# Score steps of 384 and 128 columns in one hold of PSUM banks, and another order of the attention's round

## The chip, the core and the metric

The kernel runs on one core of a Trainium2 chip. The metric is the device time of one execution in microseconds (us). The engines are named as in the profile: PE is TensorE (PEld its weight loads), DVE is VectorE, ACT is ScalarE, POOL is GpSimd, and SP is SyncE, which issues most of the DMAs. `L579` means line 579 of the kernel.

## The reference, cut to what matters

The program is a macaron block over x of 2 x 1024 rows of 256: half a feed-forward network (FFN), causal attention, and the same FFN again. The FFN with its 2:4 sparsity is left out here, since the change does not touch it.

```
q = (x @ Wq + bq) -> 32 heads of 8;  k, v = ... -> 8 heads of 8     # B = 2, T = 1024
q = q * cos + rotate_half(q) * sin;  k the same
k_rep, v_rep = repeat(k, 4), repeat(v, 4)                            # 4 query heads share one k, v
scores = einsum('bhqd,bhkd->bhqk', q, k_rep) / sqrt(8)
scores = where(kpos > qpos, -inf, scores)
attn = softmax(scores)
out = einsum('bhqk,bhkd->bhqd', attn, v_rep) @ Wo + bo
```

## The kernel before

The first FFN runs with the projections of sequence 0 between its steps, then come the attention and the second FFN. The attention is worked in 16 units, one for each sequence `b` and key head `g`; a unit has four query heads, taken as two pairs. It goes through three stages.

- **Pass 1** (`pass1`, L544) makes the scores of a block of 128 queries `qt` against up to 512 keys `kc`, with the queries on the partitions, and finds each row's maximum. The two heads of a pair lie in two strips of 64 rows of TensorE and write to the two banks of one buffer. On a diagonal block four or eight small bf16 matmuls (L567) add the causal mask. VectorE then reduces the buffer to a negated maximum for each row and head (L579). Queries 0 to 511 (half 0) need one step each, and the later ones (half 1) two, whose results `negated` (L582) joins on VectorE (L587). GpSimd splits the maximum into a high and a low part (L397, L398).
- **Shift** (`shift`) turns the split maxima with four small matmuls (L598) into rows, ScalarE copies them out (L606), and SP writes them into two extra rows of the transposed queries with four DMAs (L609). From then on a score matmul delivers the score less its row's maximum.
- **Pass 2** (`pass2`, L625 to L646) makes the scores again, for a block of 128 keys `kb` against up to 512 queries of a half `qh`, now with the keys on the partitions. ScalarE takes the exponential out of PSUM into a tile `e` (L634), GpSimd clears the masked corner of a diagonal block (L637), and `weighted` (L648) multiplies by the values (L657) into an accumulator, whose result ScalarE copies out at the end of a half.

**Holds.** The score steps of both passes, the turned q and k of the next unit (`prepare`, the op `prep`) and some other steps share one pool, `ps_big`: three buffers of two PSUM banks (2 x 512 columns of fp32), handed out in turn. A hold is the time from a step's first matmul to the end of the reduction, exponential or copy that reads it. `banks` (L540) lays a step out: with at most 256 columns both pairs of heads share a hold, and with 384 or 512 each pair has its own. A unit has 20 holds in each pass.

**The order.** A round does pass 1 of one unit, pass 2 of the unit before it and the preparation of the next. The table `order` (L720) lists its steps: `p1 8 0` is step 8 of `steps1` for pair 0, `p1 7` one for both pairs, `p2 4 1` the same of `steps2`, `av 3` the weighted sums of step 3 of pass 2, `neg1` and `shift 1` belong to half 1 of the unit before and `shift 0` to half 0 of this one; half 0's `negated` follows the last of its pass 1 steps by itself. TensorE and GpSimd execute in the order of the table (`manual_schedule`); on the other engines a scheduler sets the order. After the last round a shorter table, `last_order`, does pass 2 of the last unit, with steps of the second FFN's start between (`b`).

**Beside the rounds.** In round 0 the last down projection of the first FFN is worked in after every second pass 1 op. From round 1 the projections of sequence 1 (`project(1)`, a generator) run beside the attention: `a_step` takes its next piece after every `av`, `shift` and `prep`. A block of 512 rows has 43 pieces: 4 for the layernorm's statistics, 1 for the standard deviation, 4 to normalise, 2 transposes, 4 for a bias, and for each of four tiles one with the projection's matmuls, their bias addition on VectorE (L465) and the copy of the values, and six with one GpSimd instruction each (two of L414, then L422, L424, L427, L429). Transposes and projection take the single bank of the pool `ps_tr`, as the shift does. Before round 7, whose `prep` needs sequence 1, what is left of the generator is emitted at once:

```
if nxt is not None and nxt.b == 1:
    for _ in second:
        pass
```

Of the kernel before, what the change touches and what calls it, by code (L numbers as in the profile page):

```python
# [34 lines left out]
def macaron_kernel(  # L35
# [327 lines left out]

    ROWS = 4 * D
    STRIP = 64
    VW = D + 1

    def attention(actx, beside_first, beside_last, outs):
# [118 lines left out]
        class Unit:  # L487


            def __init__(self, b, g):  # L490
                self.b, self.g = b, g
                n = (b * NKV + g) % 3
                self.qT, self.kT = qTs[n], kTs[n]
                s = f"{b}_{g}"
                self.least = ap1.tile([P, 2, NTT, REP], FP, name=f"least{s}", tag="least", bufs=2)
                self.neg = ap1.tile([P, NQT, REP], FP, name=f"neg{s}", tag="neg", bufs=2)

            def prepare(self):

# [41 lines left out]

                return sc.rearrange("p i (s n) -> p i s n", s=len(pairs))[:, :, :, 0:n]

            def pass1(self, qt, kc, pairs):  # L544

                n = min(TB, (qt + 1) * P - kc * TB)
                diagonal = (qt // NTT) == kc
                sc = ps_big.tile(
                    [P, 2, TB], FP, name=f"s1_{self.b}_{self.g}_{qt}_{kc}_{pairs[0]}", tag="big"
                )  # L550
                to = self.banks(sc, pairs, n)

                for half in range(-1, 2 if diagonal else 0):
                    lo = max(half, 0) * STRIP
                    for s, pair in enumerate(pairs):
                        for i in range(2):
                            strip = bass.ts(i, STRIP)
                            if half < 0:
                                nc.tensor.matmul(  # L559
                                    out=to[:, i, s, :],  # L560
                                    lhsT=self.qT[strip, pair, bass.ts(qt, P)].bitcast(FR),
                                    rhs=self.kT[strip, bass.ds(kc * TB, n)].bitcast(FR),
                                    start=(s == 0),
                                    stop=not diagonal and pair == pairs[-1],
                                )
                            else:
                                nc.tensor.matmul(  # L567
                                    out=to[:, i, s, n - P + lo : n],
                                    lhsT=half_id[strip, half, :],
                                    rhs=half_mask[strip, half, lo:],  # L570
                                    start=False,
                                    stop=(half == 1 and pair == pairs[-1]),
                                )
                if qt < NTT:
                    dst = self.neg[:, qt, :]
                else:
                    dst = self.least[:, kc, qt - NTT, :]
                dst = dst[:, 2 * pairs[0] : 2 * pairs[-1] + 2].rearrange("p (s i) -> p i s", i=2)
                ins = nc.vector.tensor_reduce(dst, to, AX.X, ALU.max, negate=True)  # L579
                late["reduced"] = ins.ins  # L580

            def negated(self, half):  # L582

                s = f"{self.b}_{self.g}_{half}"
                neg = self.neg[:, bass.ts(half, NTT), :]
                if half == 1:
                    nc.vector.tensor_tensor(  # L587
                        neg, self.least[:, 0, :, :], self.least[:, 1, :, :], ALU.min
                    )
                self.ms = late["2"].tile([P, NTT, REP, 2], FR, name=f"ms{s}", tag="ms")  # L590
                split(neg, self.ms[:, :, :, 0], self.ms[:, :, :, 1], nc.gpsimd.tensor_copy)

            def shift(self, half):

                s = f"{self.b}_{self.g}_{half}"
                tr = ps_tr.tile([P, TB], FP, name=f"mT{s}", tag="tr")
                for t in range(NTT):
                    nc.tensor.matmul(  # L598
                        out=tr[0 : 2 * REP, bass.ts(t, P)],
                        lhsT=self.ms[:, t, :, :].rearrange("p i k -> p (i k)"),  # L600
                        rhs=ident_r,
                        start=True,
                        stop=True,
                    )
                mT = late["2"].tile([2 * REP, TB], FP, name=f"mrow{s}", tag="mrow")
                nc.scalar.copy(mT, tr[0 : 2 * REP, :])  # L606
                for h in range(REP):
                    lo = (h % 2) * STRIP + ROWS
                    nc.sync.dma_start(  # L609
                        out=self.qT[lo : lo + 2, h // 2, bass.ts(half, TB)],  # L610
                        in_=mT[2 * h : 2 * h + 2, :],
                    )

            def pass2(self, qh, kb, pairs):


                q0 = max(kb * P, qh * TB)
                n = (qh + 1) * TB - q0
                s = f"{self.b}_{self.g}_{qh}_{kb}_{pairs[0]}"
                sc = ps_big.tile([P, 2, TB], FP, name=f"s2_{s}", tag="big")  # L620
                to = self.banks(sc, pairs, n)
                for s, pair in enumerate(pairs):
                    for i in range(2):
                        strip = bass.ts(i, STRIP)
                        nc.tensor.matmul(  # L625
                            out=to[:, i, s, :],
                            lhsT=self.kT[strip, bass.ts(kb, P)].bitcast(FR),
                            rhs=self.qT[strip, pair, bass.ds(q0, n)].bitcast(FR),
                            start=True,
                            stop=True,  # L630
                        )
                et = late["e"].tile([P, 2, TB], FP, name=f"e_{self.b}_{self.g}_{qh}_{kb}_{pairs[0]}", tag="e")
                e = self.banks(et, pairs, n)
                nc.scalar.activation(e, to, AF.Exp, scale=SCALE)  # L634
                if kb * P == q0:

                    nc.gpsimd.affine_select(  # L637
                        out=e[:, :, :, 0:P],
                        in_=e[:, :, :, 0:P],
                        pattern=[[0, 2], [0, len(pairs)], [1, P]],  # L640
                        compare_op=ALU.is_ge,
                        fill=0.0,
                        base=0,
                        channel_multiplier=-1,
                    )
                return {2 * pair + i: e[:, i, s, :] for s, pair in enumerate(pairs) for i in range(2)}  # L646

            def weighted(self, qh, kb, es):  # L648

                n = (qh + 1) * TB - max(kb * P, qh * TB)  # L650
                last = kb == (qh + 1) * NTT - 1
                if kb == 0:
                    self.av = ps_acc.tile(
                        [P, TB], FP, name=f"av_{self.b}_{self.g}_{qh}", tag="acc"
                    )
                for i in range(REP):
                    nc.tensor.matmul(  # L657
                        out=self.av[32 * i : 32 * i + 32, TB - n : TB],
                        lhsT=vaugs[self.b][:, kb, bass.ds(self.g * VW, 32)],
                        rhs=es[i],  # L660
                        start=(kb == 0),
                        stop=last,
                    )
                if last:
                    oT = late["2"].tile([P, TB], FP, name=f"oT{self.b}_{self.g}_{qh}", tag="oT")
                    nc.scalar.copy(oT, self.av)
# [51 lines left out]


        order = """  # L720
        neg1; p2 0 0; p1 1; p2 0 1; p1 2 1; shift 1; p2 1 0; p1 3 1; prep; p1 2 0; av 11;
        p1 0; p2 1 1; p1 3 0; p2 2; p1 8 0; av 0; p2 3; p1 11 0; p2 4 1; p1 6 0; av 1;
        p2 4 0; p1 7; p2 5 1; p1 4 1; shift 0; p2 5 0; p1 9 0; av 2; av 3; p1 11 1;
        p2 6 0; p2 6 1; av 4; p1 10 1; p2 7 1; av 5; p2 7 0; p1 10 0; p2 8 0; av 6;
        p2 8 1; p1 6 1; av 7; p2 9 0; p1 4 0; p2 9 1; av 8; p2 10; p1 9 1; p1 5; av 9;
        p2 11; p1 8 1; av 10
        """
        steps1 = [(qt, kc) for qt in range(NQT) for kc in range(qt // NTT + 1)]
        steps2 = [(qh, kb) for qh in range(2) for kb in range((qh + 1) * NTT)]

        last_order = """
        neg1; p2 0 0; p2 0 1; shift 1; av 11; p2 1 0; p2 1 1; b; p2 2; av 0; b; av 1; p2 3; p2 4 0;
        p2 4 1; av 2; b; av 3; p2 5 0; p2 5 1; p2 6 0; b; p2 6 1; av 4; b; av 5; p2 7 0; p2 7 1; b;
        p2 8 0; b; av 6; b; p2 8 1; p2 9 0; b; p2 9 1; av 7; av 8; b; p2 10; b; p2 11; av 9; b;
        av 10; av 11; b
        """

        def parsed(order):
            return [(op[0], *map(int, op[1:])) for op in map(str.split, order.split(";"))]

        ops = parsed(order)
        first = max(i for i, op in enumerate(ops) if op[0] == "p1" and op[1] < NTT)
        units = [(b, g) for b in range(B) for g in range(NKV)]
        made = {}
        beside = []
# [1 line left out]
        def step(op, prev, cur, nxt):  # L747
# [5 lines left out]
                made.setdefault(arg[0], (prev, {}))[1].update(es)  # L753
            elif kind == "av" and arg[0] in made:
                unit, es = made.pop(arg[0])
                qh, kb = steps2[arg[0]]
                unit.weighted(qh, kb, es)
                if kb == (qh + 1) * NTT - 1 and unit.g == NKV - 1:
                    outs.append(output(unit.b, qh))
                    next(outs[-1])  # L760
                    if unit.b < B - 1:
# [195 lines left out]
```

## Time and profile before

| What | Value |
|---|---|
| median of three runs | 849.04 us (848.91 to 849.66) |
| the profiled execution | 848.7 us |
| its span, first to last instruction | 847.0 us |
| granted TensorE clock, mean over the span | 0.989 |
| score matmuls of both passes (L559, L625), first and last start | 183.2 and 665.3 us into the span |
| reductions of pass 1 (L579) | 320, 350.2 us busy |
| exponentials (L634) | 320, 290.3 us busy |
| selects (L637) | 192, 94.9 us busy |

The span is what the views of the trace show; the time of the execution is 1.7 us more. The page gives busy time, share of the span and number of instructions for each engine, the chain of work that ended last (which engine and line the end goes back to), and groups of instructions with their mean duration in ns and the idle time ahead of them. A line of a group reads: line, engine, operation, output<-input, shapes, count | busy us, mean ns | idle us before, and what ended it. A line of a timeline reads: start, duration, engine, line, operation, and in brackets the idle time ahead. A matmul's end is modelled, so that a TensorE that counts as busy is not one at its peak.

### The profile page before, as it was taken

To read this page: it belongs to the slowest core of one execution; us is meant where nothing else is said; L and a number is where in the kernel's file an instruction comes from. 1 tells how busy PE (TensorE), PEld (TensorE's weight loads), DVE (VectorE), ACT (ScalarE), POOL (GpSimd) and SP (SyncE) were. 2 spreads that over 40 slices of the span, in tenths; PEclk is the share of its full clock that TensorE was granted. 3 is DMA by queue.
4 is the path that set the end of the run, shared out by engine and by line. 5 is a ranking of instruction groups with operands and counts; after the bars stand their busy time and mean duration, and the time that the engine had idled before them with its cause. 6 is when DMAs were issued, how large, how long until landed. Compare 5 with 4: busy or idle time off the path is not lost.

```text
span 847.0 us, 14496 instructions
## 1 busy us (share of the span) xinstructions
PE 808.5 (95%) x5600; PEld 433.5 (51%) x5600; DVE 658.9 (78%) x870; ACT 432.4 (51%) x560; POOL 231.3 (27%) x413
## 2 busy tenths in 40 slices
PE   4999999999999999999999999999998999999997
PEld 2447575486544444454444444454434444756566
DVE  4797899888877886788888887888882579788692
ACT  1331313310676777767887787877776423222220
POOL 4001294720444464463212322123222100000000
PEclk9999999999799999999999999999999999999999
DMA  8100000022212311321233323322112100000001
GB/s 269 29 0 2 1 1 0 2 40 38 44 22 56 65 31 40 64 37 42 57 65 82 81 63 63 65 41 49 49 37 89 57 1 3 14 17 9 1 25 50
DMA packets 30997, 36.07 MB, mean 43 GB/s; under 512 B 12880, under 2 KB 20944, under 8 KB 30928
## 3 DMA queue, kind: packets, MB, share of 16 engines
q1 hardware_dynamic: 29312, 32.26, 17.0%
q10 hardware_dynamic: 1616, 2.88, 0.9%
q8 instruction: 44, 0.72, 0.3%
q14 instruction: 25, 0.20, 0.1%
HBM read 10.75 MB, written 10.75 MB: 25 GB/s over the span
## 4 chain that ended last, share of the span: by engine, by line
PE 78%; DVE 12%; ACT 6%; POOL 2%; issue 2%; DMA 0%; ACTq 0%; DVEq 0%; POOLq 0%
PE gu L247 21%; PE av L657 15%; PE o L302 11%; PE s L625 10%; PE s L559 10%; ACT e L634 4%; DVE neg L579 3%; PE pr L456 2%; PE s L567 2%; PE oo L703 2%; DVE least L579 1%; PE hT L506 1%; PE lnT L197 1%; PE mT L598 1%; POOL e L637 1%
## 5 line engine op out<-in xcount | busy, mean ns | idle before, releaser
L634 ACT ACTIVATE e<-s 128x1024 f32<-128x1024 f32 (+1 forms) x320 | 290.3, 938 | 100.4 <-PE s L625 87.4
L579 DVE TENSOR_REDUCE least<-s 128x2 f32<-128x1024 f32 (+1 forms) x224 | 252.0, 1145 | 68.0 <-PE s L559 44.0
L657 PE MATMUL av<-e,vaug 128*32 128x512 f32 (+3 forms) x1536 | 163.4, 502 | 1.6 <-POOL e L637 1.6
L637 POOL TENSOR_SCALAR_AFFINE_SELECT e<-e 128x256 f32<-128x256 f32 (+1 forms) x192 | 94.9, 495 | 251.0 <-ACT e L634 248.0
L559 PE MATMUL s<-kT,qT 64*128 64x512 f32 (+3 forms) x768 | 141.8, 395 | 12.5 <-ACT e L634 8.8
L625 PE MATMUL s<-qT,kT 64*128 64x512 f32 (+3 forms) x768 | 144.8, 410 | 2.9 <-ACT e L634 0.7
L247 PE MATMUL gu<-xnT,wg_sb 128*128 128x512 f32 x256 | 122.2, 600 | 2.1 <-DVE h L257 1.4
L625 PEld LDWEIGHTS s<-qT,kT 64*128 64x128 f32 x768 | 67.1, 188 | 105.1 <-ACT e L634 56.7
L247 PE MATMUL gu<-xnT,wu_sb 128*128 128x512 f32 x256 | 120.3, 592 | 0.0
L302 PE MATMUL o<-wd_sb,h 128*128 128x256 f32 x512 | 114.4, 381 | 0.1
L579 DVE TENSOR_REDUCE neg<-s 128x4 f32<-128x1024 f32 (+2 forms) x96 | 98.2, 1043 | 9.4 <-PE s L567 6.0
L302 PEld LDWEIGHTS o<-wd_sb,h 128*128 128x128 f32 x512 | 96.4, 190 | 17.5 <-issue 4.2
L559 PEld LDWEIGHTS s<-kT,qT 64*128 64x128 f32 x768 | 72.5, 188 | 53.8 <-ACT e L634 23.8
L255 ACT ACTIVATE sg<-gu 128x512 f32<-128x512 f32 x64 | 38.1, 595 | 117.7 <-PE gu L247 117.6
L258 ACT ACTIVATE a<-h 128x512 f32<-128x512 f32 x64 | 40.3, 630 | 99.9 <-DVE h L257 99.9
L256 DVE TENSOR_TENSOR sg<-sg,gu 128x512 f32<-128x512 f32 x64 | 43.6, 682 | 48.9 <-ACT sg L255 48.7
L247 PEld LDWEIGHTS gu<-xnT,wu_sb 128*128 128x128 f32 x256 | 48.8, 191 | 61.6 <-issue 61.6
L247 PEld LDWEIGHTS gu<-xnT,wg_sb 128*128 128x128 f32 x256 | 48.5, 192 | 55.4 <-issue 49.0
L176 POOL TENSOR_TENSOR rstd<-ve,neg_half 128x4 f32<-128x4 f32 x12 | 12.2, 1016 | 185.3 <-DVE ve L174 184.1
L567 PE MATMUL s<-half_mask,half_id 64*128 64x128 bf16 (+1 forms) x1024 | 57.4, 210 | 0.0
L657 PEld LDWEIGHTS av<-e,vaug 128*32 128x32 f32 x1536 | 32.2, 108 | 48.1 <-issue 25.8
L257 DVE TENSOR_TENSOR h<-sg,gu 128x512 f32<-128x512 f32 x64 | 44.0, 687 | 2.2
(74 smaller groups left out, 610.3 us busy)
## 6 DMA issues: line engine op xcount, KB each, us to landing
qT<-stage SPq DMA_DIRECT2D x128, 64.0 KB
avs<-oT SPq DMA_DIRECT2D x32, 256.0 KB
kT<-stage SPq DMA_DIRECT2D x128, 32.0 KB
qT<-mrow SPq DMA_DIRECT2D x128, 4.0 KB
heads<-avs SPq DMA_DIRECT2D x16, 128.0 KB
out<-x SPq DMA_DIRECT2D x8, 256.0 KB
wu_sb<-in_wu SPq DMA_DIRECT2D x2, 512.0 KB
wg_sb<-in_wg ACTq DMA_DIRECT2D x2, 512.0 KB
```

Source lines behind the costliest of these rows:

```text
L247: nc.tensor.matmul(out=gu[:, i, :], lhsT=w_sb[:, kc, gb, j, :], rhs=self.xnT[tb][:, kc, :], start=(kc == 0), stop=(kc == 1),)
L256: nc.vector.tensor_tensor(sg, sg, gu[:, 0, :], ALU.mult)
L257: nc.vector.tensor_tensor(h[:, j, :], sg, gu[:, 1, :], ALU.mult)
L258: nc.scalar.activation(a[:, j, :], h[:, j, :], AF.Abs)
L302: nc.tensor.matmul(out=o[:, i, :], lhsT=self.hms[tb][k // 4][:, k % 4, bass.ts(2 * t2 + i, P)], rhs=self.wd_sb[:, k // 4, k % 4, :], start ...
L559: nc.tensor.matmul(out=to[:, i, s, :], lhsT=self.qT[strip, pair, bass.ts(qt, P)].bitcast(FR), rhs=self.kT[strip, bass.ds(kc * TB, n)].bitc ...
L567: nc.tensor.matmul(out=to[:, i, s, n - P + lo : n], lhsT=half_id[strip, half, :], rhs=half_mask[strip, half, lo:], start=False, stop=(half ...
L579: ins = nc.vector.tensor_reduce(dst, to, AX.X, ALU.max, negate=True)
L625: nc.tensor.matmul(out=to[:, i, s, :], lhsT=self.kT[strip, bass.ts(kb, P)].bitcast(FR), rhs=self.qT[strip, pair, bass.ds(q0, n)].bitcast(F ...
L634: nc.scalar.activation(e, to, AF.Exp, scale=SCALE)
L637: nc.gpsimd.affine_select(out=e[:, :, :, 0:P], in_=e[:, :, :, 0:P], pattern=[[0, 2], [0, len(pairs)], [1, P]], compare_op=ALU.is_ge, fill=0.0,
L657: nc.tensor.matmul(out=self.av[32 * i : 32 * i + 32, TB - n : TB], lhsT=vaugs[self.b][:, kb, bass.ds(self.g * VW, 32)], rhs=es[i], start=( ...
```

## The change

Steps that fill half or three quarters of a hold are put together. In pass 1 block 2 (384 keys) shares a hold with block 0 (128), and the second step of block 6 (384) with that of block 4 (128); in pass 2 key block 1 of half 0 with 3, and key block 5 of half 1 with 7. A hold of such a kind has one pair of heads, 2 x 512 columns. The mask matmuls of the two blocks become one that writes both (256, and 2 x 64 columns). The reduction gives a maximum for every 128 columns, eight in all, and `negated` joins them: one small reduction for half 0, and two for half 1 in place of the one `tensor_tensor`. The blocks of a half then lie in the order 0, 1, 3, 2, which `shift` undoes. The exponential of a joined hold is one instruction of 1024 elements a row; its two selects stay apart. An `av` of a joined step does both key blocks. Both passes then have 18 holds a unit and 10 steps, and both order tables are new.

```diff
+    TILES = (0, 1, 3, 2)
...
-                self.least = ap1.tile([P, 2, NTT, REP], FP, name=f"least{s}", tag="least", bufs=2)
-                self.neg = ap1.tile([P, NQT, REP], FP, name=f"neg{s}", tag="neg", bufs=2)
+                self.maxima = [
+                    ap1.tile([P, REP, n], FP, name=f"maxima{s}_{n}", tag=f"max{n}", bufs=2)
+                    for n in (7, 14)
+                ]
...
-            def pass1(self, qt, kc, pairs):
+            def pass1(self, tiles, at, pairs):
...
+                ns = [min(TB, (qt + 1) * P - kc * TB) for qt, kc in tiles]
+                to = self.banks(sc, pairs, sum(ns))
...
+                            last = to[:, i, s, sum(ns) - len(ns) * P :]
+                            nc.tensor.matmul(
+                                out=last.rearrange("p (t n) -> p t n", n=P)[:, :, lo:],
+                                lhsT=half_id[strip, h, :],
+                                rhs=half_mask[strip, h, None, lo:].to_broadcast(
+                                    [STRIP, len(ns), P - lo]
+                                ),
...
+                if len(ns) == 2:
+                    dst = dst[:, :, at : at + 4]
+                    src = sc.rearrange("p i (s n) -> p i s n", n=P)
...
+                ins = nc.vector.tensor_reduce(dst, src, AX.X, ALU.max, negate=True)
...
             def negated(self, half):
+                m = self.maxima[half]
+                if half == 0:
+                    nc.vector.tensor_reduce(m[:, :, 6], m[:, :, 0:3], AX.X, ALU.min)
+                else:
+                    nc.vector.tensor_reduce(
+                        m[:, :, 10:13],
+                        m[:, :, 4:10].rearrange("p h (t k) -> p h t k", k=2),
+                        AX.X,
+                        ALU.min,
                     )
+                    nc.vector.tensor_reduce(m[:, :, 13], m[:, :, 0:4], AX.X, ALU.min)
+                neg = m[:, :, -NTT:]
...
-            def pass2(self, qh, kb, pairs):
+            def pass2(self, qh, kbs, pairs):
...
+                nc.scalar.activation(e, to, AF.Exp, scale=SCALE)
+
+                for kb, q0, n in zip(kbs, q0s, ns):
+                    if kb * P == q0:
+                        lo = 0 if kb == kbs[0] else ns[0]
+                        first = e[:, :, :, bass.ds(lo, P)]
+                        nc.gpsimd.affine_select(
...
+        neg1; p2 0 0; p1 1; p2 0 1; p1 5 0; shift 1; p2 1 1; p1 0 0; prep; p1 9 0; p2 1 0;
+        av 9; p1 0 1; p2 2; p1 2 0; av 0; p2 3 1; p1 2 1; p2 3 0; p1 9 1; p2 4 1; p1 4 1;
+        shift 0; p2 4 0; p1 5 1; av 1; p2 5 1; p1 8 1; av 2; p1 6; p2 5 0; p2 6 1; av 3;
+        p1 7 0; p2 6 0; av 4; p2 7 0; p1 7 1; p2 7 1; av 5; p1 8 0; p2 8 1; av 6; p1 3 0;
+        p2 8 0; p1 4 0; av 7; p2 9; p1 3 1; av 8
...
+        steps1 = [
+            (((2, 0), (0, 0)), 0),
+            (((1, 0),), 4),
+            (((3, 0),), 5),
+            (((4, 0),), 5),
+            (((6, 1), (4, 1)), 1),
+            (((5, 0),), 6),
+            (((5, 1),), 7),
+            (((6, 0),), 0),
+            (((7, 0),), 8),
+            (((7, 1),), 9),
+        ]
+        steps2 = [(0, (0,)), (0, (1, 3)), (0, (2,))]
+        steps2 += [(1, (kb,)) for kb in range(NTT + 1)] + [(1, (5, 7)), (1, (6,))]
...
+        neg1; p2 0 0; p2 0 1; av 9; p2 1 0; shift 1; p2 1 1; p2 2; av 0; b; av 1; b; p2 3 0; p2 3 1;
+        av 2; b; p2 4 0; p2 4 1; p2 5 0; b; av 3; b; p2 5 1; av 4; p2 6 0; p2 6 1; b; av 5; p2 7 0;
+        b; p2 7 1; b; p2 8 0; av 6; b; p2 8 1; p2 9; b; av 7; b; av 8; av 9; b
```

## The prediction

> **What bounds the kernel now.** I read the page first: busy shares, chain, groups.
>
> ```profile
> PE 808.5 (95%) x5600; PEld 433.5 (51%) x5600; DVE 658.9 (78%) x870; ACT 432.4 (51%) x560; POOL 231.3 (27%) x413
> ...
> PE 78%; DVE 12%; ACT 6%; POOL 2%; issue 2%; DMA 0%; ACTq 0%; DVEq 0%; POOLq 0%
> ```
>
> TensorE is on the chain for 78%, VectorE for 12%. Both belong partly to the attention, and an average over it hides two regimes. So I took one steady round (the rounds from 396 us on repeat every 26.68 us) and cut it at the order's `av 2`, in the table of stretches (span, then PE, PEld, DVE, ACT, POOL busy, granted clock):
>
> ```profile
> 527.03:540.66 13.63, 12.89 (x146) 7.41 (x142) 12.74 (x13) 10.70 (x14) 4.40 (x11) 1.00 0.23 37
> 540.66:553.71 13.05, 13.05 (x134) 5.19 (x130) 9.28 (x10) 10.49 (x12) 2.33 (x5) 1.00 0.29 70
> ...
> 210.70:224.30 13.60, 13.32 (x92) 8.36 (x94) 10.84 (x19) 8.03 (x9) 3.31 (x10) 0.50 0.19 31
> ```
>
> From `neg1` to `av 2` (the reduce stretch) VectorE works 12.74 of 13.63 us; from there to the next `neg1` (the matmul stretch) TensorE has no gap in 13.05. The timeline of VectorE shows the first regime: reductions end to end.
>
> ```profile
> 527.86 0.17 DVE L587 TENSOR_TENSOR neg<-least 128x16 f32<-128x16 f32 x1
> 528.13 6.33 DVE L579 TENSOR_REDUCE neg<-s 128x4 f32<-128x1024 f32 x6
> 534.38 1.22 DVE L579 TENSOR_REDUCE least<-s 128x2 f32<-128x1024 f32 x1
> 535.96 5.88 DVE L579 TENSOR_REDUCE least<-s 128x2 f32<-128x1024 f32 x5 [0.36 <-PE s L567]
> ```
>
> The third row of the table is kept for the clock: there TensorE was granted half.
>
> **The change, part by part.** A round has 40 score holds before (20 of pass 1, 20 of pass 2) and 36 after; `prep` adds one to each. Columns, score matmuls and `av` matmuls stay.
>
> *VectorE.* The groups by shape:
>
> ```profile
> L579 DVE TENSOR_REDUCE least<-s 128x2 f32<-128x1024 f32 x160 | 194.0, 1222 | 55.0 <-PE s L559 44.0 <-PE s L567 9.9
> ...
> L579 DVE TENSOR_REDUCE neg<-s 128x2 f32<-128x768 f32 x32 | 30.5, 952 | 4.0 <-PE s L567 3.3
> ...
> L579 DVE TENSOR_REDUCE least<-s 128x4 f32<-128x1024 f32 x16 | 19.6, 1224 | 2.4 <-PE s L567 1.0
> ```
>
> Two reductions of 768 and one of 512 become two of 1024, twice a round. End to end the starts lie 1.142 us (1024), 0.875 (768) and 0.60 (512) apart, so each exchange saves 0.60+2x0.875-2x1.142=0.07 us. The segments: 1024 elements into two maxima took 1222 ns, into four 1224. Eight maxima are not in the trace; the elements are the same, so there is no gain, and the bounds are 0 and, if a segment restarted the instruction, the 145 ns that is left of the 680 ns of a 512 reduction after 512x1.045 ns. I take 0, from the nearest row. The extra small reductions go against this: three a round in place of one L587 (174 ns here, 216 mean). With the gap before it, the wait behind it and the lost overlap one costs about 0.38 us of VectorE: +0.76 a round. One of the two falls into the matmul stretch, where VectorE is idle for 3.8 us.
>
> *The reduce stretch.* The order table moves work across. Before, it holds 12 reductions (nine of 1024, two of 768, one of 512: 9x1.142+2x0.875+0.60+0.17=12.8, measured 12.74) and 0.89 us of idle. After, from `neg1` to `av 1`, 10 of 1024 and two small ones: 11.42+0.34=11.76, plus the old 0.89 and 0.2 for the new one's waits: 12.85 us. By the holds: 23 in 13.63 us over three buffers are 1.78 us a hold; without the short ones about 1.87; 20 holds give 12.45. I take 12.65. ScalarE has nine exponentials (starts 0.94 apart) and 2.76 us of copies there, 11.2 us, so it is close behind.
>
> *The matmul stretch.* Before: `av` steps 7.14 us (0.996 for 512 columns, 0.783, 0.569, 0.33), masks 0.37, 18 holds 5.54, thus 0.308 a hold. After: `av 1` to `av 8` 7.6 to 7.83, 17 holds 5.23, masks 0.34: 13.25. The masks over two blocks (256 and 2x64 columns) are not in the trace; a pair of 128 columns takes 0.066 us and two pairs 0.13, so I count them as two pairs; the saving by instructions alone would be under 0.15 us a round.
>
> Round: 12.65+13.25=25.9, against 26.68: **0.8 us** saved, in 15 rounds **-12.0**. Bounds 0.2 (12.85 and 0.4 more for late exponentials) and 1.2 (12.45 and 13.05).
>
> A page of the Trainium skill speaks against it (Perfetto Trace Analysis, Identifying the Most-Contended Engine): the engine with the highest occupancy is the one to relieve, and TensorE's matmul busy time is no measure. That names VectorE, 22.02 of 26.68 us, which gets 0.6 us more; by that rule the 15 rounds would lose 9 us. The table of stretches disagrees, since VectorE binds only half of the round.
>
> *ScalarE* drops two instructions a round (0.33 us by 598+2x807 against 2x1024); in the matmul stretch this is hidden by TensorE. *GpSimd* gets 14 selects for 12, +0.42 us; it is busy 6.7 of 26.7 us, but `av 8` has two selects (0.42 each) behind `p2 8 0`: about 2.6 us after that step against 2.4 us of TensorE work between them. Cost 0 to 0.2 a round; I take 0, since kb 5 comes first. *SP*: the shift rows land 4.7 us after `shift 1` (mT at 529.15, last landing 533.85); `p2 3 1` follows 5.6 us of TensorE work later. Nothing, with 0.9 us to spare. The zeros that SP writes ahead of them wait for the unit's last pass 2 step, `p2 9` now, two steps before the round ends, as `p2 11` was. The next unit's 14 loads stay behind `prep`.
>
> *The second projection.* `a_step` advances it once for each `av`, `shift` and `prep`: 15 times a round before, 13 after. It has 2x43=86 pieces and only rounds 1 to 6: 90 before, 78 after. The rest is emitted at the head of round 7, on GpSimd ahead of the split that `shift 1` needs; the order of the changed program shows it there.
>
> ```profile
> L414 POOL TENSOR_TENSOR turn<-raw,rope_sb 128x160 f32<-128x160 f32 x32 | 21.2, 674 | 40.2 <-DVE raw L474 22.7 <-DVE raw L465 17.6
> ...
> L429 POOL TENSOR_TENSOR part<-rot,part 128x320 fp32r<-128x320 f32 x16 | 17.3, 1083 | 0.5
> L424 POOL TENSOR_TENSOR rot<-rot,turn 128x320 f32<-128x320 f32 x16 | 16.1, 1005 | 0.2
> L422 POOL TENSOR_TENSOR rot<-raw,rope_sb 128x320 f32<-128x320 f32 x16 | 14.7, 916 | 0.0
> ...
> L427 POOL CAST part<-rot 128x320 fp32r<-128x320 f32 x16 | 9.7, 604 | 0.4
> ```
>
> 2x0.674+1.083+1.005+0.916+0.604=4.96 us, after the projection's matmuls and its addition (two of 0.5, a step of 0.24, 0.56: 1.8) and before the split (0.45): 7.2 us from the round's start, and some 0.2 for two handovers. TensorE has its projection (1.0), four score steps (1.5) and their wait for a buffer (0.7) to do, 3.2 us. **+4.2**, once. Such a wait exists already:
>
> ```profile
> 636.97 0.41 PE L598 MATMUL mT<-ident_r,ms 128*8 128x128 f32 x4 [2.77 <-POOL ms L398]
> ```
>
> The clock fell to half at 637.4 for 3.4 us after that wait, and at 210.7 for 13.6 us after 3 us of sparse work; there the reduce stretch took 18.7 us for 13.6. Some 1.2 of these 5.1 us are the layernorm's instructions on VectorE, which leaves about 4. I add **+3** for round 7 (0 to 5), as the wait may also fall between two windows of the clock. The Trainium skill (TensorE: Matmul & The Clock Gate, Part 1) says that one busy window of about 3.4 us restores the clock; by it the term would be 1.7. The 13.6 us row contradicts it for this kind of work.
>
> Small terms: the eight pieces no longer in rounds 1 to 6 give **-1.5** (those rounds are 20 us longer than six steady ones, 4 of it clock; 8/86 of 16); two pieces now stand right behind `shift 1` and wait for the one transpose bank, **+1.0** (246.1 shows 0.66); round 0 ends with two holds fewer, **-1.5**; in the last unit `av 9` moves ahead of the 2.77 us wait and two holds go, **-1.0**.
>
> Sum: -12.0+4.2+3-1.5+1.0-1.5-1.0 = -7.8 on the profiled execution's 848.7 (span 847.0): 840.9. The median of the runs is 0.3 higher, so **841.0** rounded.
>
> **The rivals.** *Nothing from the rounds, so slower.* The reduce stretch is handed from VectorE to ScalarE: 11.2 us of its work plus, at each exponential that starts dry, 0.63 us (fill 0.58, release 0.05). Four dry starts make 13.7 us, and the round gains nothing; what is left is +4.2: 853. It decides where a round gains less than 0.28 us. For it: ScalarE's wait on `s`, 87.4 us in all; against: today's stretch has ten exponentials and the same copies. 0.10.
> *Within 0.2%*: a round gains 0.17 to 0.4; 849. 0.10.
> *More*: the clock holds in round 7, or round 1 loses its 13.6 us at half clock because round 0 ends denser: 848.7-12-1.5+1-1.5-1+4.2 = 837.9 for the first, 833 with both. 0.25.
> *The segments cost*: four reductions x 0.145 a round, about 15x0.3 of it in the reduce stretch: 845. 0.10.
>
> **How the numbers follow.** Forecast 0.45 (837.9 to 844). The range 831 to 850 runs from both clocks kept with 0.9 us a round to nearly nothing gained. 0.2% (1.7 us) is what a measurement of this kernel tells from no change: faster 0.80, same 0.10, slower 0.10.
>
> **What would show it.** Steady rounds of 25.9 us; a reduce stretch near 12.65 with VectorE at 11.8 busy; merged reductions at 1.22 us; one wait of TensorE of about 4 us for `ms` in round 7, with a half clock behind it. Wrong: `s` waits of ScalarE growing, or reductions into eight maxima above 1.25 us.

## The result, and the profile after

| What | Before | After |
|---|---|---|
| median on the same chip, four runs each | 848.97 us (848.30 to 849.66) | 837.42 us (835.23 to 840.35) |
| ratio, 95% interval | | 0.9866 (0.9831 to 0.9901) |
| the profiled execution, its span | 848.7, 847.0 us | 836.1, 834.4 us |
| first `shift 1` into the span | 213.9 us | 212.2 us |
| rounds 1 to 5, from one `shift 1` to the next | 152.5 us | 144.2 us |
| rounds 6 and 7 | 55.0 us | 63.8 us |
| rounds 8 to 15 | 215.6 us | 208.3 us |
| last `shift 1` to the end | 210.0 us | 206.0 us |

A round is counted here from the shift of one unit to that of the next, so a wait of round 7 for its own shift stands in the interval of round 6. The rows differ by -1.7, -8.4, +8.8, -7.3 and -4.0 us, together -12.6, the difference of the spans.

The page of the changed kernel, first the busy times, then the shares of the chain:

```profile
PE 792.0 (95%) x5344; PEld 429.0 (51%) x5344; DVE 656.4 (79%) x870; ACT 426.8 (51%) x528; POOL 236.5 (28%) x445
...
PE 79%; DVE 12%; ACT 4%; POOL 2%; issue 1%; DMA 1%; DVEq 0%; ACTq 0%; POOLq 0%
```

The shares are nearly those of before; a chain over the whole program does not show where 12 us went. VectorE's busy time fell by 2.5 us, although it has three small reductions a round for one.

The same stretches of a steady round as before, now cut at `av 1`, then the stretch of round 7 with half clock (columns as before: span, PE, PEld, DVE, ACT, POOL busy, granted clock):

```profile
548.36:560.61 12.25, 11.41 (x124) 6.72 (x120) 11.02 (x12) 10.39 (x13) 4.64 (x12) 1.00 0.22 36
534.87:548.36 13.49, 13.49 (x139) 5.63 (x137) 10.84 (x11) 10.42 (x11) 2.45 (x7) 1.00 0.29 69
388.90:399.10 10.20, 8.01 (x60) 5.42 (x60) 3.38 (x3) 4.48 (x6) 4.27 (x11) 0.50 0.13 20
```

The round is 25.74 us (26.68 before). In the second row TensorE has no gap, as before. The first row reads like the old one, VectorE 11.02 of 12.25 us, and it misleads in the same way, as the experiments show.

The reductions by shape, with their mean in ns:

```profile
L598 DVE TENSOR_REDUCE maxima<-s 128x2 f32<-128x1024 f32 x192 | 234.3, 1222 | 51.0 <-PE s L566 40.2 <-PE s L582 10.3
L598 DVE TENSOR_REDUCE maxima<-s 128x8 f32<-128x1024 f32 x64 | 78.0, 1219 | 11.9 <-PE s L582 11.8
...
L608 DVE TENSOR_REDUCE maxima<-maxima 128x12 f32<-128x24 f32 x16 | 2.9, 178 | 0.5
L614 DVE TENSOR_REDUCE maxima<-maxima 128x4 f32<-128x16 f32 x16 | 2.7, 170 | 0.5
L606 DVE TENSOR_REDUCE maxima<-maxima 128x4 f32<-128x12 f32 x16 | 2.5, 157 | 0.0
```

Eight maxima cost what two cost, and the idle time ahead of the small ones is nothing: they stand between two large ones at their bare 0.16 to 0.18 us.

The timeline of GpSimd and TensorE at the head of round 7:

```profile
386.20 1.16 POOL L415 TENSOR_TENSOR turn<-raw,rope_sb 128x160 f32<-128x160 f32 x2 [0.35 <-DVE raw L466]
...
389.71 0.86 POOL L430 TENSOR_TENSOR part<-rot,part 128x320 fp32r<-128x320 f32 x1
390.51 0.21 POOL L398 CAST ms<-maxima 128x16 fp32r<-128x16 f32 x1
...
391.09 0.59 PE L625 MATMUL mT<-ident_r,ms 128*8 128x128 f32 x4 [3.52 <-POOL ms L399]
```

The left-over pieces of the projection run ahead of the split, and TensorE's shift waits 3.52 us for it. The clock had gone to half at 388.9 and stayed there for 10.2 us (the third row of the table above).

### The profile page after: what moved, and what is told of

The parts are those of the page before. It is cut to its first block, busy times and chain, and to the rows that moved or that the text cites. A ratio compares the mean times of both kernels' runs of the same rounds, so it can differ in the third digit from the quotient of the medians.

```text
span 834.4 us, 13956 instructions
## 1 busy us (share of the span) xinstructions
PE 792.0 (95%) x5344; PEld 429.0 (51%) x5344; DVE 656.4 (79%) x870; ACT 426.8 (51%) x528; POOL 236.5 (28%) x445
## 3 DMA queue, kind: packets, MB, share of 16 engines
q10 hardware_dynamic: 1616, 2.88, 1.0%
## 4 chain that ended last, share of the span: by engine, by line
PE 79%; DVE 12%; ACT 4%; POOL 2%; issue 1%; DMA 1%; DVEq 0%; ACTq 0%; POOLq 0%
PE gu L247 22%; PE av L691 16%; PE o L302 12%; PE s L566 10%; PE s L654 10%; DVE maxima L598 4%; ACT e L664 3%; PE s L582 2%; PE pr L457 2%; PE oo L738 2%; PE hT L512 1%; PE lnT L197 1%; DVE h L287 1%; DVE h L257 1%; PE mT L625 1%
## 5 line engine op out<-in xcount | busy, mean ns | idle before, releaser
L598 DVE TENSOR_REDUCE maxima<-s 128x2 f32<-128x1024 f32 (+2 forms) x288 | 344.6, 1221 | 69.8 <-PE s L566 40.2
L664 ACT ACTIVATE e<-s 128x1024 f32<-128x1024 f32 x288 | 288.2, 1024 | 85.3 <-PE s L654 78.2
L670 POOL TENSOR_SCALAR_AFFINE_SELECT e<-e 128x256 f32<-128x256 f32 (+1 forms) x224 | 98.6, 454 | 220.5 <-ACT e L664 219.5
L691 PE MATMUL av<-e,vaug 128*32 128x512 f32 (+3 forms) x1536 | 158.7, 499 | 0.1
L566 PE MATMUL s<-kT,qT 64*128 64x512 f32 (+3 forms) x768 | 134.4, 388 | 12.1 <-ACT e L664 11.3
L654 PE MATMUL s<-qT,kT 64*128 64x512 f32 (+3 forms) x768 | 135.2, 397 | 3.3 <-DVE maxima L598 2.3
L566 PEld LDWEIGHTS s<-kT,qT 64*128 64x128 f32 x768 | 68.8, 189 | 79.3 <-ACT e L664 35.7
L691 PEld LDWEIGHTS av<-e,vaug 128*32 128x32 f32 x1536 | 33.9, 108 | 51.2 <-issue 38.0
L582 PE MATMUL s<-half_mask,half_id 64*128 64x128 bf16 (+2 forms) x768 | 51.5, 225 | 0.0
L287 DVE SCALAR_TENSOR_TENSOR h<-w,h 128x512 f32<-128x512 bf16 x64 | 44.0, 748 | 0.0
```

Of the source, the lines that this page charges most:

```text
L287: nc.vector.scalar_tensor_tensor(h[:, j, :], w[:, j, :], at, h[:, j, :], op, ALU.mult)
L566: nc.tensor.matmul(out=to[:, i, s, bass.ds(col, n)], lhsT=self.qT[strip, pair, bass.ts(qt, P)].bitcast(FR), rhs=self.kT[strip, bass.ds(kc ...
L582: nc.tensor.matmul(out=last.rearrange("p (t n) -> p t n", n=P)[:, :, lo:], lhsT=half_id[strip, h, :], rhs=half_mask[strip, h, None, lo:].t ...
L598: ins = nc.vector.tensor_reduce(dst, src, AX.X, ALU.max, negate=True)
L654: nc.tensor.matmul(out=to[:, i, s, bass.ds(col, n)], lhsT=self.kT[strip, bass.ts(kb, P)].bitcast(FR), rhs=self.qT[strip, pair, bass.ds(q0, ...
L670: nc.gpsimd.affine_select(out=first, in_=first, pattern=[[0, 2], [0, len(pairs)], [1, P]], compare_op=ALU.is_ge, fill=0.0, base=0, channel ...
```

## The experiments

Twelve versions; each ratio is to the kernel before, measured on the same chip. "Fifteen" is the new kernel with fifteen pieces of the projection a round. The three versions with joined holds in the old order have fifteen pieces too, and the `last_order` of the changed kernel, and take 2.0 to 4.5 us less than before from the last shift to the end.

| Version | Median us | Ratio, 95% interval | Steady round us |
|---|---|---|---|
| fifteen | 828.95 | 0.9753 (0.9720 to 0.9787) | 25.76 |
| joined holds, old order | 849.96 | 0.9995 (0.9981 to 1.0010) | 26.68 |
| new order, old holds | 886.95 | 1.0427 (1.0389 to 1.0465) | 29.23 |
| before, other last unit | 847.12 | 0.9981 (0.9959 to 1.0004) | 26.68 |
| joined, old order, `av 9` across | 842.27 | 0.9897 (0.9869 to 0.9924) | 26.35 |
| joined, old order, one reduction across | 852.18 | 1.0029 (1.0017 to 1.0041) | 27.01 |
| fifteen, half maxima | 820.29 | 0.9649 (0.9633 to 0.9665) | 25.38 |
| fifteen, one more reduction across | 836.16 | 0.9837 (0.9822 to 0.9851) | 26.32 |
| before, half maxima | 844.04 | 0.9938 (0.9916 to 0.9960) | 26.57 |
| fifteen, `stage` copy on VectorE | 841.45 | 0.9897 (0.9874 to 0.9920) | 26.31 |
| fifteen, late `av 9` in the last unit | 831.51 | 0.9793 (0.9763 to 0.9824) | 25.76 |
| fifteen, `oT` copies on VectorE | 832.39 | 0.9795 (0.9773 to 0.9817) | 26.07 |

### 1. Fifteen pieces a round

```diff
                 if n > 0 and op[0] in ("av", "shift", "prep"):
                     a_step()
+                if n > 0 and op in (("av", 1), ("av", 8)):
+                    a_step()
```

> The changed kernel, with a second piece of the sequence 1 projection taken after av 1 and av 8 (the two that do two key blocks), so that a round again takes 15 pieces and none is left for the head of round 7. Theory: the 3.5 us wait of TensorE for ms in round 7 and the 10.2 us at half clock behind it are caused by the eight pieces left over, so both go; the two intervals between shifts around round 7 (34.77 and 28.99 us) become about 28.3 and 25.8, the other rounds with pieces gain about 1.5 us in all, and the time is about 829 us against 837.4. Rival: the pieces cost the same wherever they stand, as GpSimd has to do them in any case, and the time stays within 835 to 838. Steady rounds stay at 25.75 us by both.

828.95 us, as the theory said. The wait of round 7 and its half clock are gone: rounds 6 and 7 take 53.7 us for 63.8. Rounds 1 to 5 get the two pieces back and are 3.1 us longer. Two tiles' projection matmuls (1.5 us each) thereby leave the interval before round 7's `shift 1`: it has three of them in the changed kernel and one here. So the two missing pieces a round took back about 8 us of the change's gain (7.8 between the spans, 834.4 and 826.6). This version beats both kernels.

### 2 and 3. The holds without the order, the order without the holds

The table of the second version is the old one with the steps renamed; where two steps became one, the later place fell away:

```
neg1; p2 0 0; p1 1; p2 0 1; p1 0 1; shift 1; p2 1 0; p1 2 1; prep; p1 0 0; p2 1 1;
p1 2 0; p2 2; p1 7 0; av 0; p1 9 0; p2 3 1; p1 5 0; av 1; p2 3 0; p1 6; p2 4 1;
p1 3 1; shift 0; p2 4 0; p1 4 0; av 2; p1 9 1; p2 5 0; p2 5 1; av 3; p1 8 1;
p2 6 1; av 4; p2 6 0; p1 8 0; p2 7 0; av 5; p2 7 1; p1 5 1; av 6; p2 8 0; p1 3 0;
p2 8 1; av 7; p2 9; p1 4 1; av 8; p1 7 1; av 9
```

> Joined holds as in the changed kernel and 15 pieces a round, but the round in the order of the kernel before: each joined step stands where its larger part stood, the smaller part is struck out. Theory (the order and the holds share the gain): its reduce stretch holds 11 reductions, 12.9 us with the small ones, so that it stays at 13.1 to 13.9 us; the round is 26.2 to 26.6 us and the time about 842. Rival one, the holds alone make the gain: a round of 25.8 us and about 829 us. Rival two, the order alone makes it: rounds of 26.7 and about 847.

849.96: a miss. Steady rounds are 26.68 us, cut at `av 2` into 13.63 and 13.05, the numbers of before. (The start and the last unit are 5.7 us shorter, and one round is 8.8 us above the steady ones, by the following.) The timeline of TensorE and SyncE there:

```profile
453.13 0.42 SPq L716 DMA_DIRECT2D heads<-avs  x1
453.65 2.53 SPq L636 DMA_DIRECT2D qT<-mrow  x4
...
456.75 1.37 PE L654 MATMUL s<-qT,kT 64*128 64x512 f32 x2 [4.57 <-DMA qT<-mrow]
```

In this table `av 9`, the last of the accumulator, stands ahead of `shift 1`; at the end of sequence 0 it sends its output DMAs down SP's queue first, the shift's rows come late, and TensorE waits 4.57 us and then runs at half clock for 10.2. In the kernel before `av 11` stood behind `prep`, and in the changed kernel `av 9` does. So this version differs from before in more than the holds; the fifth run comes nearer to that comparison.

The third version keeps the old holds and takes the new table's places for them; of the steps that the new table does not have, most stand beside their partners and two (`p2 3` with its `av 3`, and `p2 7 1`) a little later. It begins:

```
neg1; p2 0 0; p1 1; p2 0 1; p1 6 0; shift 1; p2 1 1; p1 2 0; prep; p1 11 0;
p2 1 0; av 10; av 11; p1 2 1; p1 0; p2 2; p1 3 0; av 0; p2 4 1; p1 3 1; p2 4 0;
```

> The kernel before, with 40 holds a unit, in the new order as far as its steps allow: the struck parts stand beside the larger ones, p2 3 and av 3 a little later and p2 7 1 behind av 4, as the seven exponential tiles ask for it. Theory: up to av 1 it holds 11 reductions with four short ones, 11.4 us of VectorE, and 21 holds, 12.6 us; the round is about 26.1 us and the time about 841. Rival one, holds alone: a round of 26.7 or longer and 849 or more. Rival two, order alone: 25.8 us and about 829 to 833, as no piece is left for round 7.

886.95, far off. In its steady rounds TensorE waits at the score steps for a buffer, up to 0.8 us at a time. The new table is made for 36 holds; with 40 it is much worse than the old one. How far that is the order and how far the places that I chose for those steps, this run does not tell.

### 4 and 11. The last unit

```diff
-        neg1; p2 0 0; p2 0 1; shift 1; av 11; p2 1 0; p2 1 1; b; p2 2;
+        neg1; p2 0 0; p2 0 1; av 11; p2 1 0; shift 1; p2 1 1; b; p2 2;
```

> The kernel before with one edit: in last_order av 11 and p2 1 0 stand ahead of shift 1, as av 9 does in the changed kernel. The stretch from the last shift to the end is 210.0 us before and 206.0 after the change. Theory: the shorter wait (2.77 to about 1.4 us) also keeps the clock from falling to half for 3.4 us, and this edit alone gives some 3 of these 4 us: 846. Rival: the wait moves elsewhere and the fewer holds made the 4 us: 848.5 to 849.

847.12, which the interval of the ratio does not tell from no change; the effect is read from the trace: from the last shift to the end 207.95 us for 210.01, the wait for `ms` 2.02 for 2.77, and the 3.4 us of half clock at 637.4 are gone. The reverse, in the version with fifteen pieces:

```diff
-        neg1; p2 0 0; p2 0 1; av 9; p2 1 0; shift 1; p2 1 1;
+        neg1; p2 0 0; p2 0 1; shift 1; av 9; p2 1 0; p2 1 1;
```

> The new kernel with 15 pieces a round (828.95), with av 9 of the last round back behind shift 1 in last_order. Theory (moving it ahead of the wait for ms is worth what it was worth to the kernel before, 2.06 us from the last shift to the end): the last stretch goes from 205.44 to 207.5, the total to 831.0. Rival (the 4 us come from the holds and the other steps of that table): 205.4 to 205.7, 829.

831.51; the last stretch is 207.41 us for 205.44, as expected. The wait for `ms` is longer and the half clock is back (3.4 us at 620.5):

```profile
620.10 0.41 PE L625 MATMUL mT<-ident_r,ms 128*8 128x128 f32 x4 [2.36 <-POOL ms L399]
```

With `av 9` and `p2 1 0` ahead it is 1.35. So this move of two steps is worth 2.0 us in both kernels. Here 1.0 of it is work that fills a wait; the rest, by difference, goes with the clock.

### 5, 6 and 8. Which move of the order pays

> The joined holds with the old order, but av 9 of a round moved from the round's end into the next round's reduce stretch, behind p2 1 1. Theory (what the new order brings is work taken out of the matmul stretch, where TensorE has no gap, and put where VectorE sets the pace): the matmul stretch goes from 13.05 to 12.48 us, the reduce stretch from 13.63 to 13.63 to 13.83, a round to 26.1 to 26.3; 15 x about -0.5 on 850 gives 842.5. Rival (the reduce stretch has no room either, since its own gaps are waits of TensorE that an av step does not fill): 13.63+0.57 there, rounds of 26.68, 850.

The edit moves `av 9` from the table's end to behind `p2 1 1`. 842.27, the number expected, but not by the terms expected: the round falls by 0.33 us, not 0.5 (matmul stretch 12.36, reduce stretch 14.01 us). Against the second run that gives 5 us in 15 rounds, and the rows of round 9 that no longer come as late give another 5, while rounds around a half clock of 6.8 us at the last shift take back 3.7. This is the nearest that the runs come to "the holds alone", with one `av` moved: **0.33 us a round**.

> The joined holds with the old order, but one pass 1 step (p1 4 0) moved from just ahead of av 2 to just ahead of av 4, so that the reduce stretch has ten large reductions for eleven. Theory (VectorE paces the reduce stretch): the reduce stretch loses 1.14 us (13.63 to 12.5), the matmul stretch gains a hold of 0.31 (13.05 to 13.36), a round 25.85, 15 x -0.8 on 850 gives 838. Rival (ScalarE or the three buffers pace it): the reduce stretch loses 0.35 at most, the matmul stretch gains as much, rounds of 26.6 to 26.7, 849 to 850.

```diff
-        p1 3 1; shift 0; p2 4 0; p1 4 0; av 2; ...; p2 6 1; av 4;
+        p1 3 1; shift 0; p2 4 0; av 2; ...; p2 6 1; p1 4 0; av 4;
```

> The new kernel with 15 pieces a round (828.95), with one more pass 1 step (p1 5 1) moved from the reduce stretch to just ahead of av 4. Theory (VectorE paces the reduce stretch, TensorE the other, and TensorE has room for the moved step's hold alone): reduce stretch 12.25 less 1.14 but not below TensorE's own 10.9, so 11.2 to 11.5; matmul stretch 13.48+0.31 = 13.8; rounds of 25.0 to 25.3, 15 x -0.6 gives 820. Rival (ScalarE takes over the reduce stretch at 11.9 to 12): rounds of 25.75, 829. Second rival (three holds between two av steps leave the exponentials late, 0.5 us of wait each): 832.

```diff
-        shift 0; p2 4 0; p1 5 1; av 1; ...; p2 6 0; av 4;
+        shift 0; p2 4 0; av 1; ...; p2 6 0; p1 5 1; av 4;
```

Both became slower: rounds of 27.01 (26.68) and 26.32 (25.76). The stretches of the sixth version, then of the eighth:

```profile
534.52:547.75 13.23, 11.91 (x132) 6.89 (x128) 12.36 (x13) 10.24 (x12) 3.92 (x11) 1.00 0.30 59
547.75:561.53 13.78, 13.63 (x131) 5.58 (x129) 9.68 (x10) 10.46 (x12) 3.08 (x7) 1.00 0.22 46
```

```profile
521.80:533.81 12.01, 11.16 (x122) 6.54 (x118) 10.77 (x12) 10.15 (x12) 4.62 (x12) 1.00 0.23 38
533.81:548.12 14.31, 14.25 (x142) 5.72 (x140) 11.10 (x11) 10.68 (x12) 2.44 (x7) 1.00 0.29 67
```

The reduce stretch becomes shorter by 0.40 and 0.26 us only, and the matmul stretch longer by 0.73 and 0.83. That is not the 1.1 us expected, but it does not refute VectorE as the pace either. The cut goes by TensorE, and VectorE runs behind it: the reduction of the moved step started at 546.14 in the second version, whose reduce stretch ended at 546.02, and at 553.80 in the first, whose stretch ended at 553.50. So hardly any work of VectorE left the stretch: its busy time there falls from 12.77 to 12.36 and from 11.06 to 10.77 us, by about as much as the stretch. These two runs show that the moves do not pay; what sets the pace the next two decide.

### 7 and 9. Half the maxima

```diff
-                ins = nc.vector.tensor_reduce(dst, src, AX.X, ALU.max, negate=True)
+                ins = nc.vector.tensor_reduce(
+                    dst, src[:, :, :, 0 : src.shape[-1] // 2], AX.X, ALU.max, negate=True
+                )
```

> The new kernel with 15 pieces a round (the version that took 828.95), with the pass 1 reductions reading only the first half of each segment: half of the elements are left out of the maxima. Theory (VectorE still paces the reduce stretch): a reduction takes about 0.68 us for 1.22, the reduce stretch falls from 12.25 to what TensorE needs there, 11.0 to 11.4; the matmul stretch stays at 13.48; rounds of 24.6 to 24.9, 15 x -1.0 gives 814. Rival (ScalarE with its nine exponentials and its copies, 11.2 us, paces it already): the reduce stretch keeps 12.0 us, rounds of 25.5, 825. Second rival (the reductions pace the matmul stretch too, through the buffers): that falls below 13.2 as well.

The same was done to the kernel before:

> The kernel before with its pass 1 reductions reading only the first half of their columns: half of the elements are left out of the maxima. Theory (in the old order VectorE did pace the reduce stretch, and the new order is what took that away, since the same halving gave only 0.28 us of the new reduce stretch): the reduce stretch falls from 13.63 to 12.0 to 12.5, rounds of 25.1 to 25.6, 15 x -1.3 on 850 gives 830. Rival (the exponentials that start dry and the buffers paced the old one too): reduce stretch 13.3, rounds of 26.3, 844.

These two decide what paced the reduce stretch. The kernel before with half maxima: a group of its reductions, its reduce stretch, and three of the reductions in it; then the reduce stretch of the seventh version:

```profile
L579 DVE TENSOR_REDUCE least<-s 128x2 f32<-128x512 f32 x160 | 110.3, 691 | 130.2 <-PE s L559 104.0 <-PE s L567 26.1
```

```profile
523.42:536.98 13.56, 12.51 (x147) 7.24 (x143) 7.71 (x13) 10.67 (x14) 4.40 (x11) 1.00 0.25 40
```

```profile
526.69 0.69 DVE L579 TENSOR_REDUCE neg<-s 128x2 f32<-128x512 f32 x1 [0.48 <-PE s L567]
527.90 0.56 DVE L579 TENSOR_REDUCE neg<-s 128x2 f32<-128x384 f32 x1 [0.52 <-PE s L567]
528.80 0.42 DVE L579 TENSOR_REDUCE neg<-s 128x4 f32<-128x256 f32 x1 [0.35 <-PE s L567]
```

```profile
534.48:546.47 11.99, 11.07 (x124) 6.58 (x120) 6.35 (x11) 10.42 (x13) 4.57 (x12) 1.00 0.20 34
```

Each large reduction takes 691 ns for 1222; VectorE works 7.71 us for 12.74 in the old stretch, and the stretch is 13.56 us for 13.63. In this stretch every reduction now waits for TensorE's scores. So **VectorE did not pace the kernel before**: 9 us less of it in a round gave 0.11 us. The chain of work that ended last agrees: over rounds 12 and 13 VectorE has 1.2 us a round of it before (2.3 in run 4, whose rounds have the same code), ScalarE 2.7 and TensorE 21.3; with half maxima VectorE has none, ScalarE 3.5 and TensorE 22.6. In the new order it counts a little: 11.99 for 12.27 us, 0.38 in a round. For the seventh version neither total came true (820.3, between 814 and 825), and the rival's round of 25.5 us was nearer. For the ninth the rival's 844 came true, but not by its rounds of 26.3: the spans differ by 3.6 us, of which steady rounds make 1.7 in 15; the rest lies mainly ahead of the first shift, in the first rounds and in the last.

### 10 and 12. Copies from ScalarE to VectorE

```diff
-                nc.scalar.copy(hT[0 : 2 * GW, :], tr[...])
+                nc.vector.tensor_copy(hT[0 : 2 * GW, :], tr[...])
```

> The new kernel with 15 pieces a round (828.95), with the copy of the turned q and k out of PSUM (1.01 us, once a round in the reduce stretch) on VectorE instead of ScalarE. Theory (ScalarE and its exponentials that start dry pace the new reduce stretch, VectorE has room): the reduce stretch falls from 12.27 to 11.5 to 11.9, rounds of 25.2, 15 x -0.5 gives 821. Rival (VectorE paces it): 12.27+1.1, rounds of 26.8, 844. Second rival (TensorE's own steps and the order of the buffers pace it, neither engine does): 12.2 to 12.5, 829.

```diff
-                    nc.scalar.copy(oT, self.av)
+                    nc.vector.tensor_copy(oT, self.av)
```

> The new kernel with 15 pieces a round (828.95), with the copies of the attention's accumulator out of PSUM (0.58 us, one in each stretch of a round) on VectorE instead of ScalarE. Theory (ScalarE paces the reduce stretch): 0.3 to 0.5 less there, nothing in the matmul stretch, where VectorE is idle for 2.7 us: rounds of 25.35, 823. Rival (VectorE): 0.6 more in the reduce stretch, rounds of 26.4, 838. Second rival (neither): 25.75, 829.

Both became slower than the 828.95 they start from. The reduce stretch of the tenth version:

```profile
525.49:538.28 12.79, 11.69 (x124) 6.70 (x120) 11.99 (x13) 9.44 (x12) 4.60 (x12) 1.00 0.24 38
```

ScalarE has 1.0 us less to do there and VectorE about 1.0 more, and the stretch is 0.52 longer. In the twelfth it is 0.13 longer, and the other one 0.18. VectorE has little room left in the new order, though halving its reductions was worth only 0.38 us a round; these runs load one engine while they relieve the other, so what a relief of ScalarE alone gives was not measured.

### TensorE's own time and its waits

A busy TensorE in the table of stretches hides waits, since ends of matmuls are modelled. I therefore took starts only. For each pair of neighbouring TensorE instructions of different kinds (say pass 2 with 512 columns ahead of pass 1 with 512) the tenth percentile of the distance between their starts, over the traces of before, after and ten of the versions, is taken as the first one's own time (0.332 us in this pair); what a distance has above it is a wait. Steady rounds, in us:

| Version | Own time | Waits | Round |
|---|---|---|---|
| before | 23.80 | 2.88 | 26.68 |
| before, half maxima | 23.80 | 2.77 | 26.57 |
| joined, old order, `av 9` across | 23.37 | 2.98 | 26.35 |
| after | 23.44 | 2.34 | 25.77 |
| fifteen, half maxima | 23.41 | 1.97 | 25.38 |
| fifteen, one more reduction across | 23.55 | 2.77 | 26.32 |
| new order, old holds | 24.15 | 5.08 | 29.23 |

By this reading TensorE's own steps are nearly nine tenths of the round; the joined holds shorten them by 0.4 us (64 mask matmuls a round become 48), and the new table shortens the waits by 0.6. It is a reading of the traces, not a run of its own. Waits that stand at a pair in every version are counted as own time, and the same holds in another order get 0.35 us more of it (the last row). The sizes also depend on how neighbours are paired: with runs of the same kind taken as one, two rounds of each trace give 22.9 and 3.8 us before, 22.3 and 4.1 in the fifth version, and 22.3 and 3.5 after. The direction is the same, holds shorten the steps and the table the waits, but the division of the 0.9 us is not settled. The longest idle times of TensorE in this round of the changed kernel are mostly those of pass 1 steps for a buffer that an exponential still reads:

```profile
550.06 0.50 PE L566 MATMUL s<-kT,qT 64*128 64x512 f32 x2 [0.37 <-ACT e L664]
...
551.95 0.79 PE L512 MATMUL hT<-ident_r,part 128*80 128x128 f32 x8 [0.15 <-DVE maxima L598]
...
558.01 0.50 PE L566 MATMUL s<-kT,qT 64*128 64x512 f32 x2 [0.25 <-ACT e L664]
```

The bracket gives the idle time that the modelled end leaves and its releaser: an exponential twice, a reduction once.

## Why the prediction was right or wrong

The forecast of 841.0 us lay 3.6 above the median, with the sign right and the time inside the range; the likeliest case (837.9 to 844) it missed by 0.5 us, on the fast side. Most terms came near. In the spans, with the version of fifteen pieces to separate them: rounds -14.1 (-12.0 put), pieces of the projection +7.8 (+6.7 put), round 0's tail -1.7 (-1.5 put), last unit -4.6 (-1.0 put). But the main term stands on a premise that fell, so that its nearness is in part luck.

**The rounds, -0.8 each.** Rounds 8 to 15 gained 0.91 us each, inside the bounds of 0.2 and 1.2. The cut into stretches was 12.65 and 13.25; measured 12.25 and 13.49, so that here errors cancel. The step that failed is the first: "reductions end to end", VectorE busy 12.74 of 13.63 us, read as the bound. The timeline merges neighbours: taken one by one, seven of the twelve reductions that start between 527 and 541 us have 0.05 to 0.36 us of idle ahead that TensorE's scores end. And with the reductions halved the stretch stayed (run 9). The bound by holds, 12.45 us, was the nearest of the three that it worked out: it counts the three buffers, whoever reads them. That the gain came from TensorE's own steps (where the prediction had put nothing, and under 0.15 for the masks at most) and from its waits for buffers is the reading above, without a run that divides the two; whether ScalarE, which has 2.7 us a round of the chain before and 1.0 after, could be relieved to more effect was not measured.

The rule of the Trainium skill weighed there (Perfetto Trace Analysis, Identifying the Most-Contended Engine) names VectorE for the whole round; the prediction's estimate by it was a loss of 9 us in all, and the rounds gained. The prediction doubted the rule for one half of the round only; in run 9 neither half became shorter by more than 0.07 us.

**VectorE's extra work, +0.76 a round, and the joined exchange, -0.07 each.** The small reductions were mis-sized: 0.16 to 0.18 us each, without gaps, for 0.38. VectorE's busy time in a round is 21.9 us, 22.02 before. It would not have mattered, by run 9.

**The segments at nothing.** Right: 1219 ns for eight maxima, 1222 for two. That rival is out.

**Round 7.** The mechanism was right, and so were the sizes. The wait was 3.52 us for 4.2: the five kinds of pieces took 4.19 us and not 4.96. The interval behind the wait is 28.99 us, against 25.76 with fifteen pieces: 3.2 us with the half clock, for the 3 that were put. The page on the clock (the Trainium skill, TensorE: Matmul & The Clock Gate, Part 1), by which the estimate was 1.7 us, is further off: the half clock lasted 10.2 us, three times 3.4. Rounds 6 and 7 together lost 10.05 us; the other 3.3 stand ahead of the wait, mostly two tiles' projection matmuls of 1.5 us each, and they are what rounds 1 to 5 were spared (3.1 us). For these moved pieces the prediction had put -1.5 and +1.0, a net of -0.5, for +0.2 measured.

**Round 0's tail, -1.5**: -1.7, though run 4, whose code is that of before up to there, has its first `shift 1` at 215.2 for 213.9, so that a good part can be chance. **SP, nothing**: right for this table, in which `av 9` stands behind `shift 1`. Run 2 shows the cost if that cover is gone: 4.57 us of wait and a half clock. **ScalarE and GpSimd hidden**: no steady wait of TensorE's matmuls for a select, and TensorE's matmul stretch has no gap.

**The last unit, -1.0**: -4.0 (-4.6 with fifteen pieces), the largest error. Runs 4 and 11 show 2.0 us by the steps ahead of the wait, about half of it with the clock that no longer falls; the prediction had counted the `av` step's time and left the clock out of this place, although it had quoted the half clock at 637.4. The other 2 to 2.6 us lie in the holds that go or in the rest of that table; no run tells these apart.

**The rivals.** *ScalarE takes over* needed rounds that gain less than 0.28 us; they gained 0.9, which also ends *Within 0.2%*. *More*, at 837.9 with the clock held in round 7, has the measured time and is wrong all the same: the clock fell, and the rounds and the last unit paid for it. A time alone would have confirmed it. Its other part, the half clock of round 1, lasted 10.2 us for 13.6, but that length differs between traces of the same code too.

## What to carry to other kernels

An engine that is busy for 93% of a stretch may only be keeping pace: before building on it, halve its work in one run and see whether the stretch moves. A change of holds and the order table around it are one change: with the old table the new holds gave a steady round nothing, and 0.33 us with one `av` moved; the new table on the old holds lost 2.5, and both together gained 0.9. And whoever takes steps out of a loop should look at what else is counted by those steps; here a generator that advanced with them ran late and cost 8 of 20 us.

## What the runs showed of the hardware

Away from the ends of the spans the stretches at half clock lasted 3.4, 6.8, 10.2 or 13.7 us in all these traces, multiples of 3.4. At the first rounds, where the clock is low in every version, the length differs between versions whose code up to there is the same (10.2 and 6.8 us at 211 in runs 1 and 11), and round 1 takes 30.65 and 29.69 us there. A reduction over 1024 fp32 elements a row took 1219 to 1225 ns whether it wrote two, four or eight maxima, over 512 it took 680 to 694, and over 12 to 24 elements 157 to 178.
